# First MLP product on quarters of the matmul array, with the layer norm's mean and variance products beside the out-projection

## The chip, the cores and the metric

The kernel runs on one core of one Trainium2 chip. The metric is the device time of one execution in microseconds (us). The kernel before takes 3813.03 us, the median of three runs (3812.64 to 3813.06).

## What is computed

Input `x` is 16 images of 192 channels on 64 by 64 pixels, float32 throughout. Only the last part of the reference bears on the change. Before it, a channel norm, a 1x1 projection to 384 channels, a depthwise 3x3 convolution, four directional scans along rows and columns, a second 3x3 convolution and a sigmoid gate make `mixed`, and batch statistics are taken over it. Then:

```python
mixed = gelu(batch_norm(mixed))                      # exact gelu, not the tanh form
x = x + conv1x1(mixed, out_proj_w, out_proj_b)       # 192 -> 192
h2 = ln2d(x, ln2_w, ln2_b)                           # mean and variance over the 192 channels of each pixel
m = gelu(conv1x1(h2, fc1_w, fc1_b))                  # 192 -> 768
x = x + conv1x1(m, fc2_w, fc2_b)                     # 768 -> 192
pooled = x.mean(axis=(2, 3))                         # per image and channel
taps = squeeze_excite(pooled)                        # four 3x3 taps per image and channel
out = depthwise_conv(x, taps) + bias
```

## The kernel before

The work falls into stages. A first stage reads `x`, norms it and projects it (L484 to L518). A second one does the scans and the convolutions by channel groups (L618 to L697). The third, which the change is about, runs from about 1334 us of the profile to the end.

**Chunks.** Images are taken in pairs, eight pairs in all. A pair is cut into 8 chunks of 512 pixels (8 rows), so there are 64 chunks. Each image of a pair has its own half of the 128 partitions: partitions 0 to 63 hold 64 channels of the one image, 64 to 127 the same channels of the other, and a third index `t` (0, 1, 2) counts the three blocks of 64 channels. `HALF` are the two halves.

**The order is written out by hand.** `manual_schedule` leaves each engine's instructions in the order in which the code emits them. The loop at L1036 runs `n` from -3 to 64, and its body works on several chunks at once: the MLP of chunk n, the layer norm of chunk n+1, the out-projection of chunk n+2, the gelu after batch norm of chunk n+3. For a chunk in the middle, TensorE gets these blocks:

- `first(n, k)`, k = 0, 1, 2 (L922): two of the six blocks of 128 hidden channels. Each output `pf` is two PSUM banks of 512 columns, one for each image. For each `t` there are two matmuls, one for each image: 64 contraction rows by 128 output columns (L930). ScalarE then applies gelu to both banks at once (L933).
- `out_proj(n + 2, t)`, t = 0, 1, 2 (L857): four matmuls of 64 rows by 64 columns (L865) and four of 128 rows by 64 columns (L869), each on 256 columns of data. VectorE adds bias and residual (L872), and at t = 1 and t = 2 it sums the three channel blocks into `sm` (L876, L883, L885), so that the mean takes a contraction over 64 and not over 192.
- `second(n, k)` (L936): 128 rows by 64 columns (L827, in the helper `both`), into three banks of tag `f2`.
- `mean` (L887), called by `center(n + 1)` as `ps_m` and by `normalize(n + 1)` as `ps_v`: four matmuls of 64 by 64 (L892) with a matrix that holds 1/192.

In the trace each matmul of the code has two records; 24 records are a block of `first` or `second`, 8 are one of L865, L869 or L892.

The sequence on TensorE in one turn of the loop is: first 0, out_proj 0, second 2 of the chunk before, `ps_m`, first 1, out_proj 1, second 0, `ps_v`, first 2, out_proj 2, second 1.

**Buffers.** `pf`, `ps_o`, `ps_m` and `ps_v` share the tag `f1`, which has two buffers of two PSUM banks each. They alternate, so a block that writes one waits for the readers of the one before the last. There are 11 such tiles in a turn.

**The other engines.** `center` subtracts the mean (VectorE, L901), `squares` squares on ScalarE (L908) and sums over the channel blocks on VectorE (L909, L883, L885), `normalize` takes the square root on ScalarE (L918), the reciprocal (L919) and the product (L920) on VectorE. `final` adds the MLP's result to the image (L951). `unmix` transposes blocks (L239), `bn_gelu` is L854 and L855. Of a pair that has ended, `pooled`, `squeeze` and `excite` make the taps, and 12 `piece`s (one L990 on ScalarE, three L65 on VectorE, one output transfer each) do its convolution, two in a turn, during six of the next pair's eight chunks. Gelu and square root need different tables of ScalarE: the trace has a table load before each L918 and another before the L933 that follows.

Of the kernel before, what the change touches and what calls it, by code (L numbers as in the profile page):

```python
# [21 lines left out]
F32 = mybir.dt.float32  # L22
AF = mybir.ActivationFunctionType
# [8 lines left out]
CH = 512  # L32
HCH = CH // 2
CR = CH // HW
# [21 lines left out]
def conv_block_kernel(ctx: ExitStack, tc: tile.TileContext, x, prm, w_in, w_out, w_fc1, b_fc1, w_fc2, w1, bn1, w2, out):  # L56
    nc = tc.nc
# [5 lines left out]
    HALF = (slice(0, 64), slice(64, 128))  # L63
# [25 lines left out]
    eps6 = cp.tile([128, 1], F32, tag="eps6", name="eps6")  # L89
# [7 lines left out]
    wf1 = k2.tile([128, 3, NFC * 128], F32, tag="wf1", name="wf1")  # L97
# [6 lines left out]
    b1 = k2.tile([RED, 4], F32, tag="b1", name="b1")  # L104
    s1 = k2.tile([RED, 1], F32, tag="s1", name="s1")
    pv = k2.tile([128, 2, NPRM], F32, tag="pv", name="pv")

    mean64 = k2.tile([128, 64], F32, tag="mean64", name="mean64")
# [137 lines left out]
    with ExitStack() as stage:  # L246
# [3 lines left out]
        lo = slice(0, 64)  # L250
# [289 lines left out]
        for dst, src in ((pt3, prm), (w0, w_in)):  # L540
            v = src.rearrange("(t p) n -> p t n", p=64)
# [254 lines left out]
    k3 = ctx.enter_context(tc.tile_pool(name="k3", bufs=1))  # L796
# [12 lines left out]
    ys = {n // 2: spare[:, (n - 2) * 3 * CH:n * 3 * CH].rearrange("p (t w e) -> p t w e", t=3, w=2) for n in range(2, NCH, 2)}  # L809
    ys[0] = y_low  # L810

    pool2 = k3.tile([128, 3, 2], F32, tag="pool2", name="pool2")

    hp2 = ctx.enter_context(tc.tile_pool(name="h2", bufs=2))
    wp = ctx.enter_context(tc.tile_pool(name="w2", bufs=1))
    op = ctx.enter_context(tc.tile_pool(name="o2", bufs=2))
    ps2 = ctx.enter_context(tc.tile_pool(name="ps2", bufs=1, space=PSUM))

    n_ch = n_pairs * NCH
    NPS = NFC // 2  # L820
    st = [dict() for _ in range(n_ch)]
# [7 lines left out]
    def img_of(n):  # L829
        r = 1 + (n % NCH) * CR  # L830
        return ximg[(n // NCH) % n_img][:, :, r:r + CR, 1:1 + HW]

    def rows(a):
        return a.rearrange("p (h w) -> p h w", w=HW)
# [19 lines left out]
        nc.scalar.activation(mx[:, 0:2], mx[:, 0:2], AF.Gelu, bias=bn_bi[:, 0:1], scale=bn_sc[:, 0:1])  # L854
        nc.scalar.activation(mx[:, 2], mx[:, 2], AF.Gelu, bias=bn_bi[:, 1:2], scale=bn_sc[:, 1:2])  # L855

    def out_proj(n, t):  # L857
        s, img = st[n], img_of(n)

        ps = ps2.tile([128, 2, CH], F32, tag="f1", name="ps_o", bufs=2)[:, :, 0:CH // 2]  # L860
        cols = lambda a: a.rearrange("p r (k w) -> p r k w", k=2)

        for wh, qr in enumerate(HALF):
            for i, q in enumerate(HALF):
                nc.tensor.matmul(ps[q, wh], wo2[qr, 64 * t:64 * t + 64], s["mx"][qr, 2, 256 * i:256 * i + 256],  # L865
                                 start=True, stop=False)
        for wh in range(2):
            for i, q in enumerate(HALF):
                nc.tensor.matmul(ps[q, wh].rearrange("p (r w) -> p r w", w=32), wo[:, 64 * t:64 * t + 64],  # L869
                                 cols(rows(s["mx"][:, i]))[:, :, wh], start=False, stop=True)  # L870
        for wh in range(2):
            nc.vector.scalar_tensor_tensor(cols(img[:, t])[:, :, wh], ps[:, wh].rearrange("p (r w) -> p r w", w=32),  # L872
                                           pt3[:, t, OUTB:OUTB + 1], cols(rows(s["x2"][:, t]))[:, :, wh], ALU.add, ALU.add)
        if t == 1:
            s["sm"] = hp2.tile([128, 3, HCH], F32, tag="sm", name="sm", bufs=1)
            nc.vector.tensor_add(rows(s["sm"][:, 0:2].rearrange("p k n -> p (k n)")), img[:, 0], img[:, 1])  # L876
        if t == 2:
            sm = s["sm"]
            sums(*(rows(a) for a in (sm[:, 0], sm[:, 2], sm[:, 0], sm[:, 1])), img[:, 2, 0:CR // 2], img[:, 2, CR // 2:CR])

    def sums(o0, o1, a0, a1, b0, b1):

        nc.vector.tensor_add(o0, a0, b0)  # L883
        for i, q in enumerate(HALF):
            nc.vector.tensor_add(o1[HALF[1 - i]], a1[q], b1[q])  # L885

    def mean(name, s0, s1):  # L887

        ps = ps2.tile([128, 2, CH], F32, tag="f1", name=name, bufs=2)[:, :, 0:HCH]
        for k, a in enumerate((s0, s1)):  # L890
            for i, q in enumerate(HALF):
                nc.tensor.matmul(ps[HALF[i ^ k], k], mean64[q], a[q], start=True, stop=True)  # L892
        return ps

    def center(n):
        s, img = st[n], img_of(n)
        pm = mean("ps_m", s["sm"][:, 0], s["sm"][:, 2])
        h = hp2.tile([128, 3, CH], F32, tag="h2", name="h2")
        hr = CR // 2
        for k in range(2):  # L900
            nc.vector.tensor_sub(h.rearrange("p t (h w) -> p t h w", w=HW)[:, :, k * hr:(k + 1) * hr], img[:, :, k * hr:(k + 1) * hr],  # L901
                                 rows(pm[:, k]).unsqueeze(1).broadcast_to([128, 3, hr, HW]))
        s.update(h=h)

    def squares(n):
        s = st[n]
        sq = wp.tile([128, 3, CH], F32, tag="sq2", name="sq2")
        nc.scalar.activation(sq, s["h"], AF.Square)  # L908
        nc.vector.tensor_add(sq[:, 0], sq[:, 0], sq[:, 1])  # L909
        v = sq.rearrange("p t (k n) -> p t k n", k=2)  # L910
        sums(v[:, 0, 0], v[:, 1, 0], v[:, 0, 0], v[:, 0, 1], v[:, 2, 0], v[:, 2, 1])
        s.update(sq=v)

    def normalize(n):
        s = st[n]
        pw = mean("ps_v", s["sq"][:, 0, 0], s["sq"][:, 1, 0])
        rs = hp2.tile([128, CH], F32, tag="rs2", name="rs2", bufs=1)
        nc.scalar.activation(rs.rearrange("p (k n) -> p k n", k=2), pw, AF.Sqrt, bias=eps6)  # L918
        nc.vector.reciprocal(rs, rs)  # L919
        nc.vector.tensor_mul(s["h"], s["h"], rs.unsqueeze(1).broadcast_to([128, 3, CH]))  # L920

    def first(n, k):  # L922

        s = st[n]
        s["gl", k] = []
        for m in (2 * k, 2 * k + 1):
            pf = ps2.tile([128, 2, CH], F32, tag="f1", name="ps_f1", bufs=2)
            for t in range(3):
                for i, q in enumerate(HALF):
                    nc.tensor.matmul(pf[:, i], wf1[q, t, 128 * m:128 * m + 128], s["h"][q, t],  # L930
                                     start=(t == 0), stop=(t == 2))
            gl = wp.tile([128, 2, CH], F32, tag="gl", name="gl", bufs=4)
            nc.scalar.activation(gl, pf, AF.Gelu, bias=bf1[:, m:m + 1])  # L933
            s["gl", k].append(gl)
# [48 lines left out]
    def dynamic(p, g, t):  # L983
        xi, taps, r = ximg[p % n_img], pst[p]["taps"], g * GR
        o = op.tile([128, GR, HW], F32, tag="o", name="o")
        for k in range(NTAP):
            src = xi[:, t, r + k // 3:r + k // 3 + GR, k % 3:k % 3 + HW]
            w = taps[:, t, k:k + 1]
            if k == 0:
                nc.scalar.activation(o, src, AF.Identity, bias=pt3[:, t, BIAS:BIAS + 1], scale=w)  # L990
            else:
                stt(o, src, w, o)
        for i, q in enumerate(HALF):
            nc.gpsimd.dma_start(ov[2 * p + i, 64 * t:64 * t + 64, r * HW:(r + GR) * HW], o[q].rearrange("p h w -> p (h w)"))  # L994
# [31 lines left out]
    def at(f, n, *a):  # L1026
        if n is not None and 0 <= n < n_ch:
            f(n, *a)
# [3 lines left out]
    def piece():  # L1032
        if pieces:
            dynamic(*pieces.pop(0))

    for n in range(-3, n_ch + 1):  # L1036
        ended = (n - 1) // NCH if n >= NCH and (n - 1) % NCH == NCH - 1 else None
        if n + 5 < NCH and (n + 5) % 2 == 0:
            load_y(n + 5, ys[(n + 5) // 2], (nc.sync, nc.gpsimd) if n == -3 else (nc.gpsimd,))
        if n == -3:  # L1040
            border(ximg[0])
        if n == 0:
            nc.vector.memset(pool2, 0.0)
        if n == NCH - 3:
            border(ximg[1])

        early_, late_ = (n + 3, None) if n != -1 else (None, 2)
        at(load, n + 3)
        at(unmix, early_)
        at(load_mixed, n + 4)  # L1050
        at(first, n, 0)
        at(bn_gelu, early_)
        at(out_proj, n + 2, 0)
        piece()
        at(second, n - 1, NPS - 1)
        at(center, n + 1)
        at(final, n - 1)
        if ended is not None:
            pooled(ended)
        at(first, n, 1)  # L1060
        if ended is not None:
            squeeze(ended)
        at(out_proj, n + 2, 1)
        at(squares, n + 1)
        at(second, n, 0)
        piece()
        at(normalize, n + 1)
        at(first, n, 2)
        if ended is not None:
            excite(ended)  # L1070
            if ended < n_pairs - 1:
                pieces += [(ended, g, t) for g in range(NG) for t in range(3)]
        at(out_proj, n + 2, 2)
        at(second, n, 1)
        at(unmix, late_)
        at(bn_gelu, late_)
# [64 lines left out]
```

## Time and profile before

| what | value |
|---|---|
| span of the profiled execution | 3814.8 us |
| TensorE busy with matmuls | 3764.5 us (99%), 25,644 matmul records |
| weight loads (beside the matmuls) | 1719.9 us (45%) |
| VectorE busy | 2665.5 us (70%) |
| ScalarE busy | 1779.2 us (47%) |
| first MLP product, L930 | 4,608 records, 1050.2 us |
| second MLP product, L827 | 4,608 records, 1021.6 us |
| out-projection, L869 and L865 | 1,536 records each, 210.0 and 129.9 us |
| mean and variance products, L892 | 512 records each, 43.0 and 43.7 us |

Busy time is the time in which at least one instruction of the engine (or of the group) was running. Matmuls overlap, so a busy TensorE is not yet TensorE at its peak; how far apart the starts of successive matmuls are tells more. "idle before" in a group's row is the time in which the engine had nothing running just ahead of the group's instructions.

### The profile page before, as it was taken

How to read it: one execution, taken by the hardware profiler on the slowest of the kernel's cores; microseconds unless marked ns; L12 is line 12 of the kernel's file. 1: busy time of each engine (PE TensorE's matmuls, PEld its weight loads, DVE VectorE, ACT ScalarE, POOL GpSimd, SP SyncE). 2: the span in 40 equal slices, each digit the busy share in tenths (PEclk: the TensorE clock that was granted, in tenths of full speed). 3: DMA queues.
4: the chain of work that ended last, by engine and by line, in shares of the span. 5: the costliest groups of instructions: out<-in, count | busy, mean ns of one | idle time of the engine just before them, and what ended most of it. 6: DMA issues, size and time to landing. Idle time of an engine off the chain costs nothing.

```text
span 3814.8 us, 61825 instructions
## 1 busy us (share of the span) xinstructions
PE 3764.5 (99%) x25644; PEld 1719.9 (45%) x25644; DVE 2665.5 (70%) x4132; ACT 1779.2 (47%) x1881; POOL 420.1 (11%) x683
## 2 busy tenths in 40 slices
PE   8999999999999899999999999999999999999998
PEld 5666656555555433333333333333333333333333
DVE  6887776999999964557656656756665765674753
ACT  3433434888888733333434333433433433343433
POOL 2434332010110110000000000000000000000000
PEclk9999999999999999999999999999999999999999
DMA  6899998999999741112212212222222221221212
GB/s 163 239 252 237 272 275 261 282 280 273 284 275 269 208 89 34 43 39 72 75 48 61 75 56 64 61 67 58 70 56 64 72 65 45 76 71 42 67 36 72
DMA packets 308391, 491.15 MB, mean 129 GB/s; under 512 B 46656, under 2 KB 202640, under 8 KB 308112
## 3 DMA queue, kind: packets, MB, share of 16 engines
q1 hardware_dynamic: 250064, 295.14, 29.2%
q0 software_dynamic: 57152, 190.94, 18.9%
q8 instruction: 203, 3.33, 0.4%
q10 hardware_dynamic: 896, 1.12, 0.1%
q14 instruction: 76, 0.62, 0.1%
HBM read 284.91 MB, written 197.92 MB: 127 GB/s over the span
## 4 chain that ended last, share of the span: by engine, by line
PE 96%; DMA 1%; DVE 1%; ACT 0%; issue 0%; POOL 0%; SPq 0%; ACTq 0%; POOLq 0%
PE ps_f L930 27%; PE ps_f L827 26%; PE ps_pj L512 13%; PE ps_l L662 11%; PE ps_d L618 6%; PE ps_o L869 5%; PE ps_o L865 3%; PE ps_xt L484 2%; PE ps_v L892 1%; PE ps_m L892 1%; DMA xa<-in_x_dram 1%; PE ps_k L827 0%; DMA ximg<-mixed_d 0%; DMA mixed_d<-mid 0%; DVE v L653 0%
## 5 line engine op out<-in xcount | busy, mean ns | idle before, releaser
L930 PE MATMUL ps_f<-h,wf 64*128 64x512 f32 x4608 | 1050.2, 601 | 4.0 <-DVE h L920 3.3
L827 PE MATMUL ps_f<-gl,place 128*64 128x512 f32 x4608 | 1021.6, 592 | 0.0
L933 ACT ACTIVATE gl<-ps_f,bf 128x1024 f32<-128x1024 f32 x384 | 427.6, 1114 | 1163.7 <-PE ps_f L930 1162.9
L930 PEld LDWEIGHTS ps_f<-h,wf 64*128 64x128 f32 x4608 | 434.3, 187 | 563.0 <-issue 560.8
L872 DVE SCALAR_TENSOR_TENSOR ximg<-ps_o,pt,low 128x256 f32<-128x256 f32 x384 | 168.3, 480 | 626.5 <-PE ps_o L869 623.7
L827 PEld LDWEIGHTS ps_f<-gl,place 128*64 128x64 f32 x4608 | 330.7, 137 | 579.8 <-issue 537.6
L512 PE MATMUL ps_pj<-wi,xa 64*128 64x384 f32 x3072 | 516.0, 489 | 4.9 <-DVE stg L517 4.8
L65 DVE SCALAR_TENSOR_TENSOR o<-ximg,taps,o 128x1024 f32<-128x1024 f32 x252 | 323.7, 1285 | 85.9 <-ACT o L990 78.4
L512 PEld LDWEIGHTS ps_pj<-wi,xa 64*128 64x128 f32 x3072 | 293.6, 188 | 199.3 <-issue 12.8
L994 POOL DMA_DIRECT2D out_dram<-o x168 | 87.9, 528 | 2134.3 <-DVE o L65 2131.5
L919 DVE RECIPROCAL rs<-rs 128x512 f32<-128x512 f32 x64 | 214.3, 3348 | 64.9 <-ACT rs L918 64.9
L653 DVE TENSOR_TENSOR_SCAN v<-tab,q 128x1024 f32<-128x1024 f32 x96 | 218.3, 2274 | 7.5 <-DMA pg_d<-mid 7.5
L655 DVE TENSOR_TENSOR_SCAN v<-tab,q 128x1024 f32<-128x1024 f32 x96 | 217.5, 2266 | 0.0
L869 PE MATMUL ps_o<-low,wo 128*64 128x256 f32 x1536 | 210.0, 395 | 0.0
L518 ACT ACTIVATE stg<-ps_pj,rsa 128x384 f32<-128x384 f32 x128 | 120.0, 941 | 191.3 <-PE ps_pj L512 179.8
L641 ACT ACTIVATE tab<-mask,dec_b 128x1024 f32<-128x1024 f32 x192 | 209.0, 1137 | 0.0
L518 ACT ACTIVATE mid<-ps_pj,rsa 128x384 f32<-128x384 f32 x128 | 120.7, 943 | 180.9 <-PE ps_pj L512 175.0
L901 DVE TENSOR_TENSOR h<-ximg,ps_m 128x768 f32<-128x768 f32 x128 | 116.1, 948 | 98.7 <-PE ps_m L892 98.7
L491 DVE BATCH_NORM_STATS2 st<-ps_xt 128x6 f32<-128x192 f32 x512 | 173.2, 338 | 17.0 <-PE ps_xt L484 16.8
L239 DVE STREAM_TRANSPOSE low<-low 128x512 f32<-128x512 f32 x174 | 167.7, 1015 | 2.0 <-issue 0.3
L472 POOL DMA_DIRECT2D xa<-in_x_dram x192 | 119.8, 630 | 363.1 <-PE ps_pj L512 285.1
L951 DVE SCALAR_TENSOR_TENSOR ximg<-ps_f,pt,ximg 128x512 f32<-128x512 f32 x192 | 134.0, 747 | 36.2 <-PE ps_f L827 35.8
(198 smaller groups left out, 4020.0 us busy)
## 6 DMA issues: line engine op xcount, KB each, us to landing
low<-in_x_dram SPq DMA_DIRECT2D x128, 384.0 KB
out_dram<-o POOLq DMA_DIRECT2D x168, 256.0 KB, 3.7
mid<-pg_d SPq DMA_DIRECT2D x8, 4096.0 KB
low<-mixed_d SPq DMA_DIRECT2D x116, 256.0 KB
low<-pg_d SPq DMA_DIRECT2D x7, 4096.0 KB
pg_o<-pg_d SPq DMA_DIRECT2D x7, 4096.0 KB
xa<-in_x_dram POOLq DMA_DIRECT2D x192, 128.0 KB, 5.8
xa<-in_x_dram SPq DMA_DIRECT2D x192, 128.0 KB
```

The source lines that it names most:

```text
L65: nc.vector.scalar_tensor_tensor(o, in0, scalar, in1, ALU.mult, ALU.add, **kw)
L512: nc.tensor.matmul(ps[i], pixels(n, t, g)[q], wi[q, t].rearrange("p g k c -> p (g k c)"), start=(t == 0), stop=(t == 2))
L518: nc.scalar.activation(stag[blk][1][:, :, j], ps[1], AF.Copy, scale=rs[:, g, 1:2])
L618: nc.tensor.matmul(dst(ps[o, ih]), mats[g % 2]["dm"][q, di + 1, :, ch], src(s["pg"][q, :, 0, ch]), start=(di == 0), stop=stop)
L653: nc.vector.tensor_tensor_scan(vf, tab, q, 0.0, ALU.mult, ALU.add)
L655: nc.vector.tensor_tensor_scan(vf[:, ::-1], tab[:, ::-1], q[:, ::-1], 0.0, ALU.mult, ALU.add)
L662: nc.tensor.matmul(dst(bst[k]["ps"][i][o]), lm_of(g)[q, m, :, c], src(q, ih), start=start, stop=stop)
L827: nc.tensor.matmul(ps[q], w(i), rhs(i), start=start, stop=stop)
L869: nc.tensor.matmul(ps[q, wh].rearrange("p (r w) -> p r w", w=32), wo[:, 64 * t:64 * t + 64], cols(rows(s["mx"][:, i]))[:, :, wh], start=Fa ...
L919: nc.vector.reciprocal(rs, rs)
L930: nc.tensor.matmul(pf[:, i], wf1[q, t, 128 * m:128 * m + 128], s["h"][q, t], start=(t == 0), stop=(t == 2))
L933: nc.scalar.activation(gl, pf, AF.Gelu, bias=bf1[:, m:m + 1])
```

## The change

The first MLP product, the mean and the variance are put into one form with the first half of the out-projection: 64 rows by 64 columns, four of them on the four quarters of the array. The mean and the variance are placed directly before the out-projection's quarters, and each shares a PSUM tile with it (the mean or variance in the upper 256 columns, the out-projection in the lower), so that three blocks of the same form follow each other. Since the tile is shared, both are read only when both are written. The layer norm's mean is taken one place earlier in the turn, and the variance before second(n, 0) and not after it. The sums that feed them are cut into four parts of 64 partitions, laid out for the quarters. After the square root, an activation of one column calls gelu, so that gelu's table is fetched before it is needed.

```diff
+    warm = k3.tile([128, 1], F32, tag="warm", name="warm")
-        ps = ps2.tile([128, 2, CH], F32, tag="f1", name="ps_o", bufs=2)[:, :, 0:CH // 2]
+    def products(n, t):
+        if not -2 <= n < n_ch - 1:
+            return
+        ps = ps2.tile([128, 2, CH], F32, tag="f1", name="ps_o", bufs=2)
+        pm, po = ps[:, :, HCH:CH], ps[:, :, 0:HCH]
+        if t < 2:
+            at(mean, n + 1, pm, ("sm", "sq")[t])
+        at(out_proj, n + 2, t, po)
+        if t == 0:
+            at(center, n + 1, pm)
+        if t == 1 and 0 <= n + 1 < n_ch:
+            st[n + 1]["pw"] = pm
+        at(residual, n + 2, t, po)
...
-        nc.vector.tensor_add(o0, a0, b0)
-        for i, q in enumerate(HALF):
-            nc.vector.tensor_add(o1[HALF[1 - i]], a1[q], b1[q])
+        lo, hi = HALF
+        for o, a, b in ((o0[lo], a0[lo], b0[lo]), (ox[lo], a0[hi], b0[hi]), (ox[hi], a1[lo], b1[lo]), (o1[hi], a1[hi], b1[hi])):
+            nc.vector.tensor_add(o, a, b)
...
-        ps = ps2.tile([128, 2, CH], F32, tag="f1", name=name, bufs=2)[:, :, 0:HCH]
-        for k, a in enumerate((s0, s1)):
-            for i, q in enumerate(HALF):
-                nc.tensor.matmul(ps[HALF[i ^ k], k], mean64[q], a[q], start=True, stop=True)
-        return ps
+        s0, s1, sx = st[n][what]
+        for k, kinds in enumerate(((s0, sx), (sx, s1))):
+            for i, a in enumerate(kinds):
+                nc.tensor.matmul(ps[HALF[i], k], mean64[HALF[k]], a[HALF[k]], start=True, stop=True)
...
-        pw = mean("ps_v", s["sq"][:, 0, 0], s["sq"][:, 1, 0])
...
+        nc.scalar.activation(rs.rearrange("p (k n) -> p k n", k=2), s["pw"], AF.Sqrt, bias=eps6)
+        nc.scalar.activation(warm, eps6, AF.Gelu)
...
-                    nc.tensor.matmul(pf[:, i], wf1[q, t, 128 * m:128 * m + 128], s["h"][q, t],
-                                     start=(t == 0), stop=(t == 2))
+                    for j, o in enumerate(HALF):
+                        m0 = 128 * m + 64 * j
+                        nc.tensor.matmul(pf[o, i], wf1[q, t, m0:m0 + 64], s["h"][q, t], start=(t == 0), stop=(t == 2))
...
         at(first, n, 0)
         at(bn_gelu, early_)
-        at(out_proj, n + 2, 0)
+        products(n, 0)
         piece()
+        at(squares, n + 1)
         at(second, n - 1, NPS - 1)
-        at(center, n + 1)
         at(final, n - 1)
...
         at(first, n, 1)
+        products(n, 1)
...
-        at(out_proj, n + 2, 1)
-        at(squares, n + 1)
         at(second, n, 0)
         piece()
         at(normalize, n + 1)
...
-        at(out_proj, n + 2, 2)
+        products(n, 2)
         at(second, n, 1)
```

In the turn after the change TensorE's sequence is: first 0, mean, out_proj 0, second 2 of the chunk before, first 1, variance, out_proj 1, second 0, first 2, out_proj 2, second 1. The tag `f1` has nine tiles in a turn.

## Prediction before the changed kernel was run

> **What bounds the kernel now.** I read the shares by engine first, then the chain of waits, then the costliest groups: TensorE is busy 99%, is 96% of the chain, and the groups of the last stage hardly idle. Nothing waits, so what is left to gain is the rate within the busy time.
>
> ```profile
> PE 3764.5 (99%) x25644; PEld 1719.9 (45%) x25644; DVE 2665.5 (70%) x4132; ACT 1779.2 (47%) x1881; POOL 420.1 (11%) x683
> PE 96%; DMA 1%; DVE 1%; ACT 0%; issue 0%; POOL 0%; SPq 0%; ACTq 0%; POOLq 0%
> L930 PE MATMUL ps_f<-h,wf 64*128 64x512 f32 x4608 | 1050.2, 601 | 4.0 <-DVE h L920 3.3
> L827 PE MATMUL ps_f<-gl,place 128*64 128x512 f32 x4608 | 1021.6, 592 | 0.0
> ```
>
> For the rate I took the timeline of TensorE in a middle chunk (start, length, records). Starts of neighbouring rows give each block's true length; the lengths in the rows overlap.
>
> ```profile
> 2527.63 5.42 PE L930 MATMUL ps_f<-h,wf 64*128 64x512 f32 x24
> 2532.98 0.66 PE L865 MATMUL ps_o<-low,wo 64*64 64x256 f32 x8
> 2533.57 1.08 PE L869 MATMUL ps_o<-low,wo 128*64 128x256 f32 x8
> 2534.49 5.32 PE L827 MATMUL ps_f<-gl,place 128*64 128x512 f32 x24
> 2539.74 0.66 PE L892 MATMUL ps_m<-sm,mean 64*64 64x256 f32 x8
> 2540.33 0.70 PE L930 MATMUL ps_f<-h,wf 64*128 64x512 f32 x2
> ```
>
> Blocks: L930 5.35 us, L865 0.59, L869 0.92, L827 5.25, L892 0.59. Single records show the grain: two matmuls (halves) or four (quarters) start within 20 ns, and the next group follows after 0.429 us at 512 columns, 0.2155 at 256. So 24 records in halves are 12 groups, 5.15 us; eight in quarters two groups, 0.43; eight in halves four, 0.86. The rest sits at **changes of form** only. The first group of a new form comes about 0.10 us late (0.11 after a 256-column group). The second comes late again, by 0.052 where the new form has 64 columns (0.267, not 0.215), by 0.105 where it has 128 (0.534, not 0.429). L869 to L827 changes line, not form, and costs nothing.
>
> A chunk has 11 changes: L930 to L865 three at 0.148 us (0.096+0.052), L865 to L869 three at 0.163, L827 to L892 two at 0.152, L892 to L930 two at 0.216, L827 to L930 one at 0.205. Sum 1.874. Add 36+36 groups of 0.429 and 22 of 0.2155: 35.63. Together 37.50. The period is 37.55 us in 14 of 61 middle chunks, 37.73 in 40, 39.25 in the 7 that also run squeeze and excite. The missing bits are two waits: 0.05 us of L865 on the gelu behind a table load, and in the 40 chunks with pieces 0.17 us of L930's second tile on center (L901). The first is visible here, gelu ending at 2520.81 and L865 at 2520.87, 0.05 later than its pattern:
>
> ```profile
> 2518.41 1.28 ACT L933 ACT_TABLE_LOAD   x1 [2.11 <-PE ps_f L930]
> 2519.70 1.11 ACT L933 ACTIVATE gl<-ps_f,bf 128x1024 f32<-128x1024 f32 x1
> 2520.87 0.66 PE L865 MATMUL ps_o<-low,wo 64*64 64x256 f32 x8
> ```
>
> **What the Trainium skill says.** "TensorEngine Tiling (Array Packing)", section Key Properties: changing the tiling mode, not just the tile, drains TensorE. The trace agrees, at 0.10 us. "TensorE: Matmul & The Clock Gate", section LDWEIGHTS: a load takes its columns divided by 1.2 ns, 53 ns for 64 and 107 for 128. The second group's lag of 52 and 105 ns is just that, so I read it as a weight load with no matmul to hide behind. "ScalarE: Activation LUTs", section What ACT_TABLE_LOAD costs: some 1283 ns a load; the trace has 1.28 us.
>
> **The change, part by part.**
>
> *First product on quarters.* 2,304 matmuls become 4,608 (9,216 records, 30,252 in all), in groups of four instead of two: the same 36 groups a chunk. Their price stands in the stage before, where L662 does 64x64 by 512 in quarters. Six groups in 2.57 us (four of them of 504 columns) and four in 1.71 are 0.428 each, also across a change of line:
>
> ```profile
> 1208.92 2.75 PE L662 MATMUL ps_l<-q,mid 64*64 64x512 f32 x24
> 1211.49 1.90 PE L662 MATMUL ps_l<-v,mid 64*64 64x512 f32 x16
> 1213.20 2.79 PE L618 MATMUL ps_d<-mid,dm 64*64 64x512 f32 x40
> ```
>
> So: no gain and no loss within the block. The doubled loads lie beside matmuls, as L662's do.
>
> *Changes of form.* First, mean and L865 now have one form. Left are L865 to L869 three times at 0.163 and L827 to first three times at 0.10+0.052=0.152 (the price of L827 to L892): 0.945 us instead of 1.874. Gain 0.93 a chunk.
>
> *Waits removed.* The table load moves behind the square root, where ScalarE would idle some 5 us (square root done at 22.0 in the count below, next gelu at 27.5): gain 0.05. The one-column activation (nearest row 0.29 us) hides there too. Center is now followed by second (5.25) and the first tile of first (2.6) before its buffer is wanted: gain 0.17 in 40 chunks.
>
> *Waits added.* Center and residual (VectorE), and the square root (ScalarE), stand until out_proj's end, up to 1.5 us later than the mean or variance alone. Counting from first 0's start in a chunk with pieces: mean 5.20, L865 5.63, L869 6.17, second 7.09. Center (1.81) runs 7.3 to 9.1, residual (0.88) to 10.0, a piece (3.93) to 13.95; ScalarE does two gelus, bn_gelu, the piece's L990 (to 9.5) and the square (1.47, to 11.0). The sums (0.69 + four of 0.42) end at 16.35, and the variance wants them at 17.55: 1.2 us of slack. Queued behind are final (to 18.8; second wants its banks from 19.4), residual 1 and the second piece (to 25.1), reciprocal 3.35 and product 1.76 (to 30.3; the next first wants h at 36.6). `f1` tiles: out_proj's wait for gelus that end 1.2 us ahead, first's for residuals further ahead. All hidden, the variance by least.
>
> *Four-part sums.* Four of 0.42 us instead of 0.43+0.84, twice a chunk: +0.43 each, 55 us more VectorE over all, in the slack just counted.
>
> A middle chunk is then 35.63+0.945=36.58 us, to the 37.55, 37.73 or 39.25 of before. Gains: 14x0.97=13.6, 40x1.15=46.0, and for the seven (36.58+1.65 for squeeze and excite) 7x1.02=7.1. The last two chunks, which have no out-projection, give 0.6. Sum 67.3.
>
> *Start of the stage,* where no MLP hides the chain from sum to first product. Before, the mean ran at 1342.5 us and the first product began at 1356.81. After: sums 0.43 longer, the mean followed by out_proj (1.5) before center may start; squares likewise 0.43 longer, the variance followed by another out_proj (1.5), and residual 1 ahead of the reciprocal. That shifts the first product by 3.6 us. One table load (1.28) then no longer precedes bn_gelu: about +2.3 remains. Between 2 and 5; I take +3.5, with chunk 0 counted in and its gain left out.
>
> Forecast: 3813.0-67.3+3.5=**3749.2 us**.
>
> **Rivals.** (a) *The variance waits.* If sums come 2 us later than counted (pieces held by output buffers, transposes by loads), the slack of 1.2 is overdrawn by 0.8 in 40 chunks: +32, 3781. For it: smallest slack, long VectorE queue. Against: VectorE is busy only about 65% here. (b) *Only part of the drain goes.* If second-group loads stay exposed at the joins first to mean and first to out_proj, five of 0.052 in 64 chunks: +17, 3766. Against: L662 to L618 joins at 0.428. (c) *Slower.* If in this code the four loads of a group don't hide, each of 36 groups takes 0.052 more: 1.87 a chunk, 120 us, 3869. Against: L662 again, though its weights are laid out otherwise. (d) *Quicker:* the start costs nothing and squeeze changes form less often: 3743.
>
> **How the numbers follow.** Forecast 0.70, (a) 0.10, (b) 0.08, (c) 0.05, (d) 0.07. The range, 3741 to 3770, takes in the forecast with the start's bounds, (b) and (d), and a mild (a). Faster by over 0.2% (below 3805.4): all but (c) and a heavy (a), 0.94; the same 0.01; slower 0.05.
>
> **What would show it.** First at 0.429 a group in fours, block 5.20; mean and L865 0.2155 a group with no lag before them; six lags a chunk; period 36.6 for pieces and none alike; no table load ahead of L933. A TensorE wait on the sums of squares would show (a), groups of 0.48 us (c).

## The result, and the profile after

The changed kernel takes 3756.72 us (median of 4 runs, 3752.6 to 3758.05), against 3813.05 for the kernel before beside it (median of 4, 3812.64 to 3823.58). The medians lie 56 us apart. The ratio, into which every run goes, is 0.9844, with a 95% interval of 0.9825 to 0.9863. The forecast was 3749.2, the range 3741 to 3770. In a second comparison, in which both kernels ran slower, the changed kernel took 3763.53 us, the kernel before 3822.01, and the ratio was 0.9841 (0.9825 to 0.9857).

Medians carry the first two stages, which the change does not touch and which vary: the first out-projection begins between 1331.28 and 1341.10 us in the twelve profiles of this study, all with the same code ahead of it. Why they vary is open. Below, therefore, I compare pieces of the third stage from the traces; there the 61 middle chunks together repeat to within 0.01 us in the profiles that have the same code for them.

The page of the changed kernel, its busy times and costliest groups:

```profile
PE 3696.1 (99%) x30252; PEld 1651.4 (44%) x30252; DVE 2716.6 (72%) x4260; ACT 1794.8 (48%) x1945; POOL 420.2 (11%) x683
L955 PE MATMUL ps_f<-h,wf 64*64 64x512 f32 x9216 | 1035.9, 595 | 6.8 <-DVE h L943 6.7
L828 PE MATMUL ps_f<-gl,place 128*64 128x512 f32 x4608 | 1022.2, 592 | 0.0
```

TensorE is as busy as before, 99%, with 4,608 records more and 68 us less. The first product (now L955) has twice the records in 14 us less. Most of the gain is not in these rows; it is between the blocks. The timeline of TensorE in a middle chunk (start, length, records):

```profile
2535.49 5.38 PE L955 MATMUL ps_f<-h,wf 64*64 64x512 f32 x48
2540.69 0.61 PE L916 MATMUL ps_o<-sm,mean 64*64 64x256 f32 x8
2541.12 0.61 PE L883 MATMUL ps_o<-low,wo 64*64 64x256 f32 x8
2541.66 1.08 PE L887 MATMUL ps_o<-low,wo 128*64 128x256 f32 x8
2542.58 5.32 PE L828 MATMUL ps_f<-gl,place 128*64 128x512 f32 x24
2547.83 5.38 PE L955 MATMUL ps_f<-h,wf 64*64 64x512 f32 x48
```

By the differences of the starts: first 5.20 us (5.35 before), mean 0.43 (0.59), L883 0.54 (0.59), L887 0.92, second 5.25. Single records show first's groups of four 0.429 us apart, the mean's following in 0.216, and lags only where second turns to first (0.529, then 0.480) and L883 to L887 (0.326, then 0.267): six a chunk.

Where the time went, between fixed points of the two traces (us):

| stretch | before | after | difference |
|---|---|---|---|
| start of the span to first out-projection | 1334.10 | 1331.28 | -2.82 (code unchanged) |
| first out-projection to first MLP product | 22.71 | 30.16 | +7.45 |
| chunk 0 | 35.93 | 34.97 | -0.96 |
| chunks 1 to 61 | 2309.83 | 2243.24 | -66.59 |
| last two chunks, to the last second product | 69.72 | 69.16 | -0.56 |
| the rest | 42.47 | 41.99 | -0.48 |

### The profile page after: what moved, and what is told of

Its sections match the earlier page's. It is cut to its first block, busy times and chain, and to the rows that moved or that the text cites. A ratio compares the mean times of both kernels' runs of the same rounds, so it can differ in the third digit from the quotient of the medians.

```text
span 3750.8 us, 71230 instructions
## 1 busy us (share of the span) xinstructions
PE 3696.1 (99%) x30252; PEld 1651.4 (44%) x30252; DVE 2716.6 (72%) x4260; ACT 1794.8 (48%) x1945; POOL 420.2 (11%) x683
## 4 chain that ended last, share of the span: by engine, by line
PE 97%; DVE 1%; DMA 1%; ACT 0%; issue 0%; SPq 0%; ACTq 0%; POOL 0%; DVEq 0%
PE ps_f L955 27%; PE ps_f L828 26%; PE ps_pj L512 13%; PE ps_l L662 11%; PE ps_d L618 7%; PE ps_o L887 5%; PE ps_xt L484 2%; PE ps_o L883 2%; PE ps_o L916 2%; DMA xa<-in_x_dram 1%; PE ps_k L828 0%; DVE v L653 0%; DVE v L655 0%; DMA out_dram<-ol 0%; PE ps_d L1038 0%
## 5 line engine op out<-in xcount | busy, mean ns | idle before, releaser
L955 PE MATMUL ps_f<-h,wf 64*64 64x512 f32 x9216 | 1035.9, 595 | 6.8 <-DVE h L943 6.7
L955 PEld LDWEIGHTS ps_f<-h,wf 64*64 64x64 f32 x9216 | 334.5, 133 | 693.8 <-issue 642.6
L923 DVE TENSOR_TENSOR h<-ximg,ps_o 128x768 f32<-128x768 f32 x128 | 116.4, 951 | 425.5 <-PE ps_o L887 417.2
L893 DVE SCALAR_TENSOR_TENSOR ximg<-ps_o,pt,low 128x256 f32<-128x256 f32 x384 | 168.0, 480 | 267.5 <-PE ps_o L887 264.9
L65 DVE SCALAR_TENSOR_TENSOR o<-ximg,taps,o 128x1024 f32<-128x1024 f32 x252 | 323.2, 1282 | 8.7 <-ACT o L1014 2.6
L887 PE MATMUL ps_o<-low,wo 128*64 128x256 f32 x1536 | 210.2, 395 | 0.0
```

Source lines behind the costliest of these rows:

```text
L65: nc.vector.scalar_tensor_tensor(o, in0, scalar, in1, ALU.mult, ALU.add, **kw)
L955: nc.tensor.matmul(pf[o, i], wf1[q, t, m0:m0 + 64], s["h"][q, t], start=(t == 0), stop=(t == 2))
```

## The experiments

Times are medians. "Chunks" is the stretch of chunks 1 to 61 in the profile, "start" the one from first out-projection to first MLP product. Intervals are those of the ratio to the kernel before, run beside it. Compare by ratio: the kernel before took 3817.99 us beside `quarters_only`, `move_only`, `twice_the_changes` and `own_tile`, 3822.01 beside `no_early_table`, `early_table_only`, `start_apart` and the repeat, and 3817.24 beside `quarters_and_table`.

| kernel | us | ratio (95%) | chunks | start |
|---|---|---|---|---|
| before | 3813.05 | 1 | 2309.83 | 22.71 |
| changed | 3756.72 | 0.9844 (0.9825 to 0.9863) | 2243.24 | 30.16 |
| quarters_only | 3783.16 | 0.9916 (0.9900 to 0.9933) | 2278.12 | 22.24 |
| early_table_only | 3817.48 | 0.9987 (0.9980 to 0.9993) | 2307.05 | 22.23 |
| quarters_and_table | 3770.47 | 0.9867 (0.9844 to 0.9890) | 2265.43 | 22.67 |
| move_only | 3797.31 | 0.9947 (0.9931 to 0.9964) | 2279.98 | 29.81 |
| no_early_table | 3773.94 | 0.9872 (0.9857 to 0.9887) | 2255.57 | 31.41 |
| twice_the_changes | 3814.77 | 0.9992 (0.9985 to 0.9998) | 2299.79 | 32.17 |
| own_tile | 3890.71 | 1.0189 (1.0174 to 1.0204) | 2376.87 | 27.27 |
| start_apart | 3755.44 | 0.9822 (0.9808 to 0.9837) | 2243.24 | 24.32 |
| start_mean_apart | 3754.45 (one run) | none taken | 2243.24 | 29.41 |
| changed, again | 3763.53 | 0.9841 (0.9825 to 0.9857) | 2243.24 | 31.62 |

### Is it the number of changes of form?

`twice_the_changes` is the changed kernel with the out-projection's two parts exchanged:

```diff
-        for wh, qr in enumerate(HALF):
-            for i, q in enumerate(HALF):
-                nc.tensor.matmul(ps[q, wh], wo2[qr, 64 * t:64 * t + 64], s["mx"][qr, 2, 256 * i:256 * i + 256],
-                                 start=True, stop=False)
...
-                                 cols(rows(s["mx"][:, i]))[:, :, wh], start=False, stop=True)
+                                 cols(rows(s["mx"][:, i]))[:, :, wh], start=True, stop=False)
+        for wh, qr in enumerate(HALF):
+            for i, q in enumerate(HALF):
+                nc.tensor.matmul(ps[q, wh], wo2[qr, 64 * t:64 * t + 64], s["mx"][qr, 2, 256 * i:256 * i + 256],
+                                 start=False, stop=True)
```

> The changed kernel with the two parts of the out-projection in the other order: first the matmuls of 128 rows by 64 columns, then the quarters. The same matmuls, and 12 changes of form a chunk in place of 6. Theory: 0.163 + 0.152 us more at each of three places, 0.945 us a chunk in 62 chunks: 59 us more than the changed kernel, about 3816, no gain left over the kernel before. Rival (the gain is in the waits that fell away, not in the form): about 3757.

The chunks grew by 56.55 us, 0.927 a chunk where 0.945 were counted, and the gain over the kernel before was nearly gone. The matmuls are the same; six more changes of form cost some 0.154 us each. The timeline of TensorE shows where they lie:

```profile
2508.04 5.38 PE L955 MATMUL ps_f<-h,wf 64*64 64x512 f32 x48
2513.24 0.61 PE L916 MATMUL ps_o<-sq,mean 64*64 64x256 f32 x8
2513.78 1.08 PE L883 MATMUL ps_o<-low,wo 128*64 128x256 f32 x8
2514.80 0.66 PE L887 MATMUL ps_o<-low,wo 64*64 64x256 f32 x8
2515.39 5.37 PE L828 MATMUL ps_f<-gl,place 128*64 128x512 f32 x24
2520.69 5.38 PE L955 MATMUL ps_f<-h,wf 64*64 64x512 f32 x48
```

By the starts, the halves, now between two quarter blocks, take 1.02 us and not 0.92, the quarters 0.59 and not 0.54, second 5.30 and not 5.25, the variance 0.54 and not 0.43.

### One part alone

`quarters_only` is the kernel before with this edit:

```diff
-                    nc.tensor.matmul(pf[:, i], wf1[q, t, 128 * m:128 * m + 128], s["h"][q, t],
-                                     start=(t == 0), stop=(t == 2))
+                    for j, o in enumerate(HALF):
+                        m0 = 128 * m + 64 * j
+                        nc.tensor.matmul(pf[o, i], wf1[q, t, m0:m0 + 64], s["h"][q, t], start=(t == 0), stop=(t == 2))
```

> The kernel before with the first product on quarters and nothing else moved. Theory (a change of form costs 0.15 to 0.22 us, a change of block in the same form nothing): the mean and variance blocks, out of place as they are, now have the form of the blocks behind them, so six changes a chunk are left, as in the changed kernel: 0.93 us a chunk less. In the 40 chunks with pieces the 0.22 us won between mean and first are lost again in the wait on center, since VectorE sets its end. 21x0.93 + 40x0.71 + 0.5 = 48 us: about 3765. The start of the stage stays as before. Rival 1 (the mean and variance have to stand beside the out-projection for the gain): only first to out-projection and second to first get cheaper, 0.60 us a chunk: about 3776. Rival 2 (each change of block costs, whatever the form): about 3810.

Measured 3783, and 31.7 us won in the chunks where I expected 48. The total lies near that of rival 1, but the blocks speak against it. All the changes of form went that the theory names: from mean to first it takes 0.48 us and not 0.59, so that lag is gone, and the kernel has six changes a chunk. But two waits, and the lags behind them, took most of 25 us of the 57 (61 times the 0.93 of the expectation) back. The largest of TensorE's waits in the third stage (total, times, longest):

```profile
PE ps_f L932 <- DVE h L901: 11.5, 40, 0.6
```

It is first's second tile waiting for center, 40 times; the blocks tell its full size, since the last matmuls still run while it begins. One such chunk (first 1 in its two tiles of 24 records, then the out-projection; most rows of the other engines are left out):

```profile
2633.70 3.93 DVE L65 SCALAR_TENSOR_TENSOR o<-ximg,taps,o 128x1024 f32<-128x1024 f32 x3 [1.87 <-ACT o L991]
2636.47 2.75 PE L932 MATMUL ps_f<-h,wf 64*64 64x512 f32 x24
2637.55 1.81 DVE L901 TENSOR_TENSOR h<-ximg,ps_m 128x768 f32<-128x768 f32 x2
2639.51 2.81 PE L932 MATMUL ps_f<-h,wf 64*64 64x512 f32 x24 [0.28 <-DVE h L901]
2642.10 0.64 PE L865 MATMUL ps_o<-low,wo 64*64 64x256 f32 x8
```

In chunks with pieces VectorE comes to center only after a piece (L65), whose own start hangs on the gelus of first 0, so that nearly everything TensorE saves from first 0 to first 1 (0.148 and 0.216 us) is waited away: first 1 took 5.63 us there, not 5.15 (before 5.52, not 5.35), and the out-projection behind it 0.03 more. The second loss does not show among the waits at all: the third first block took 5.33 us, not 5.15, until the gelu behind its table load was done, and the out-projection after it 0.05 more.

`early_table_only` and `quarters_and_table` add to the kernel before, and to `quarters_only`, these lines:

```diff
+    warm = k3.tile([128, 1], F32, tag="warm", name="warm")
...
+        nc.scalar.activation(warm, eps6, AF.Gelu)
```

> The kernel before with the one-column gelu after the square root and nothing else. Theory: 0.05 us less in 61 chunks and 1.28 us less at the start of the stage: 4.3 us faster than the kernel before, about 3809. Rival: no difference.

> The kernel before with the first product on quarters and the one-column gelu after the square root; mean and variance stay where they were. Theory (without the lag of a change of form behind first's third block, the late table costs some 0.23 us a chunk and not 0.05; the wait on center in chunks with pieces stays): from chunk 1 to chunk 62 2278.1 us of the kernel with quarters alone become 2266, between 2262 and 2268; that kernel in all about 12 us faster. Rival (the table is worth 3 us here, as in the halves): 2275.

In halves the early table is worth 2.8 us over the chunks, in quarters 12.7, both as expected; the third first block is 5.15 us again. `no_early_table` takes those lines out of the changed kernel:

> The changed kernel without the one-column gelu after the square root. Theory: the load of gelu's table stands ahead of the first gelu after first's third block again; the out-projection waits 0.05 us for it in some 61 chunks, 3.0 us, and batch norm's gelu at the start of the stage gets its 1.28 us back: 4.3 us slower than the changed kernel run beside it. Rival (the one-column activation only fills idle time of ScalarE): no difference.

It lost 12.3 us in the chunks and not 3: 0.23 in each of 54 chunks, and nothing in the seven with squeeze and excite. I had priced the late table by what it cost before, 0.05 us; there the lag of the change of form ran at the same time and covered most of the wait. With the change gone, the wait stands bare: first 2 takes 5.38 us, not 5.20, and the out-projection behind it 0.59, not 0.54.

`move_only` is the changed kernel with the two `first` lines of `quarters_only` put back:

> The changed kernel with the first product in halves of 64 rows by 128 columns again. Theory: nine changes a chunk: first to mean or out-projection 3x0.148, out-projection's two parts 3x0.163, second to first 3x0.205, 1.55 us; no wait on center or gelu. A chunk is 37.18 us: 30 us won over the chunks, of which the longer start of the stage (7.4 us, less 1.3) takes 6: about 3789. Rival (the gain is in sharing the tile and in the place of the mean): most of the 56 us, about 3760.

29.9 us won in the chunks against 30 counted, in all 3797 against 3789; the medians of this comparison are all some 5 us higher (the kernel before 3818 beside it).

One after the other the parts give: quarters 31.7, early table 12.7, mean and variance moved 22.2, together 66.6 us. The last step removes no change of form. It removes the waits on center: in `quarters_and_table` the 40 chunks with pieces take 37.09 us and those without 36.58, in the changed kernel both take 36.58, which is 20 of the 22 us. The rest is in the seven chunks with squeeze and excite (38.50 and 38.25 us). The move does two things at once: the mean comes one place earlier on TensorE, and center comes ahead of the piece on VectorE. Which of the two removes the wait was not run apart.

### Is sharing the tile needed?

`own_tile` gives mean and variance a tile of their own:

```diff
-        ps = ps2.tile([128, 2, CH], F32, tag="f1", name="ps_o", bufs=2)
-        pm, po = ps[:, :, HCH:CH], ps[:, :, 0:HCH]
-        if t < 2:
+        pm = None
+        if t < 2 and 0 <= n + 1 < n_ch:
+            pm = ps2.tile([128, 2, CH], F32, tag="f1", name="ps_m", bufs=2)[:, :, 0:HCH]
             at(mean, n + 1, pm, ("sm", "sq")[t])
+        ps = ps2.tile([128, 2, CH], F32, tag="f1", name="ps_o", bufs=2)
+        po = ps[:, :, 0:HCH]
```

> The changed kernel with mean and variance in a PSUM tile of their own, so that center and the square root need not wait for the out-projection. Theory (sharing saves a buffer): with 11 tiles in a turn on two buffers the out-projection has to wait for the gelu of the first product's second tile, which ends some 1.4 us after that product; 0.97 us idle at t=0 and t=1, 1.95 us a chunk in 62 chunks, less some 2 us at the start of the stage: about 3876, slower than before. Rival (reading only when all is written costs something in every chunk): a bit faster than the changed kernel, 3745 to 3755.

3891 us, slower than the kernel before. TensorE:

```profile
2532.18 0.61 PE L918 MATMUL ps_m<-sm,mean 64*64 64x256 f32 x8
2533.66 0.66 PE L885 MATMUL ps_o<-low,wo 64*64 64x256 f32 x8 [0.86 <-ACT gl L959]
2534.25 1.08 PE L889 MATMUL ps_o<-low,wo 128*64 128x256 f32 x8
```

The out-projection starts 1.48 us after the mean, not 0.43: it waits for the gelu of the tile before the mean's. That is 1.05 us, and 0.05 more in the block itself (0.59 for 0.54), twice a chunk: 2.19 us a chunk, 1.95 expected. Reading both only when both are written costs nothing in a chunk (the changed kernel's blocks keep their counted lengths there); two more tiles in a turn on the same two buffers do.

### Why the start grew

At the start of the stage nothing hides the chain from sums to first product. ScalarE there, first the kernel before, then the changed one:

```profile
1346.00 1.48 ACT L908 ACTIVATE sq<-h 128x1536 f32<-128x1536 f32 x1 [9.25 <-PE ps_o L869]
1347.50 1.28 ACT L918 ACT_TABLE_LOAD   x1
1350.80 0.69 ACT L918 ACTIVATE rs<-ps_v,eps 128x512 f32<-128x512 f32 x1 [2.01 <-PE ps_v L892]
```

```profile
1345.19 1.48 ACT L930 ACTIVATE sq<-h 128x1536 f32<-128x1536 f32 x1 [11.26 <-DVE h L923]
1354.13 1.28 ACT L939 ACT_TABLE_LOAD   x1 [7.46 <-DVE ximg L893]
1355.43 0.69 ACT L939 ACTIVATE rs<-ps_o,eps 128x512 f32<-128x512 f32 x1
```

Before, the square root's table was loaded right after the square, while VectorE summed. Now the load stands until VectorE's residual has read the same tile, and then lies bare ahead of the square root. VectorE, again the kernel before first:

```profile
1348.73 0.85 DVE L885 TENSOR_TENSOR sq<-sq 64x256 f32<-64x256 f32 x2
1351.52 3.35 DVE L919 RECIPROCAL rs<-rs 128x512 f32<-128x512 f32 x1 [1.94 <-ACT rs L918]
```

```profile
1343.26 1.82 DVE L923 TENSOR_TENSOR h<-ximg,ps_o 128x768 f32<-128x768 f32 x2 [2.19 <-PE ps_o L887]
...
1347.44 1.77 DVE L908 TENSOR_TENSOR sq<-sq 64x256 f32<-64x256 f32 x4
1353.18 0.88 DVE L893 SCALAR_TENSOR_TENSOR ximg<-ps_o,pt,low 128x256 f32<-128x256 f32 x2 [3.97 <-PE ps_o L887]
1354.09 0.69 DVE L897 TENSOR_TENSOR sm<-ximg 128x512 f32<-128x512 f32 x1
1356.15 3.35 DVE L942 RECIPROCAL rs<-rs 128x512 f32<-128x512 f32 x1 [1.37 <-ACT rs L939]
```

From the end of the sums (1349.21) to the reciprocal it is 6.94 us, against 1.94 before: 3.97 until variance and out-projection are done, 0.9 for the residual, 1.28 for the load, 0.7 for the square root. Center begins 2.2 us after its sums, against 0.8 before.

Two causes lie in this, and `own_tile` tells them apart, for it leaves the order of the changed kernel and only gives mean and variance tiles of their own. There ScalarE loads the table right behind the square again (two rows of ScalarE, then two of VectorE):

```profile
1347.40 1.48 ACT L932 ACTIVATE sq<-h 128x1536 f32<-128x1536 f32 x1 [9.93 <-DVE h L925]
1348.90 1.28 ACT L941 ACT_TABLE_LOAD   x1
...
1355.27 0.88 DVE L895 SCALAR_TENSOR_TENSOR ximg<-ps_o,pt,low 128x256 f32<-128x256 f32 x2 [3.76 <-PE ps_o L889]
1356.79 3.35 DVE L944 RECIPROCAL rs<-rs 128x512 f32<-128x512 f32 x1
```

So the bare load comes of the shared tile. The larger part does not: the reciprocal still begins 5.28 us after the sums (1351.51), because VectorE has the residual of the out-projection ahead of it in its order. `start_apart` changes both, the tile and the order, for chunk 0 alone:

```diff
+        alone = n == -1 and t < 2
+        if alone:
+            pm = ps2.tile([128, 2, CH], F32, tag="f1", name="ps_m", bufs=2)[:, :, 0:HCH]
+            mean(0, pm, ("sm", "sq")[t])
+            if t == 0:
+                center(0, pm)
+            else:
+                st[0]["pw"] = pm
+                normalize(0)
         ps = ps2.tile([128, 2, CH], F32, tag="f1", name="ps_o", bufs=2)
...
-        at(normalize, n + 1)
+        at(normalize, n + 1 if n >= 0 else None)
```

> The changed kernel, with mean and variance of chunk 0 in tiles of their own, centered and normalized before the out-projection of chunk 1 that stands beside them; all later chunks share tiles as before. Theory (the start of the stage grew by 7.4 us because center and square root wait for out-projections that no MLP hides, and because the table of the square root is loaded only after the residual): the first MLP product begins some 7 us earlier after the first out-projection, 23 us and not 30; 6 us faster than the changed kernel, about 3750. Rival (what is longer is hidden behind batch norm's gelu of chunk 2): no difference.

The start fell to 24.32 us, and ScalarE loads the table beside the sums again:

```profile
1353.41 1.48 ACT L941 ACTIVATE sq<-h 128x1536 f32<-128x1536 f32 x1 [9.66 <-DVE h L934]
1354.92 1.28 ACT L950 ACT_TABLE_LOAD   x1
1358.63 0.69 ACT L950 ACTIVATE rs<-ps_m,eps 128x512 f32<-128x512 f32 x1 [2.43 <-PE ps_m L927]
```

From the first out-projection to the end it takes 2413.64 us, the changed kernel 2419.52 and 2420.87: 6 to 7 us less. The medians, 3755.44 and 3763.53, say 8, though the intervals of the two ratios overlap. Counted from the first out-projection on, it is the fastest of these versions. `start_mean_apart` does the mean's half only:

> The changed kernel, with only the mean of chunk 0 in a tile of its own and centered ahead of chunk 1's first out-projection; its variance shares a tile as in the changed kernel. Theory: of the 7.4 us by which the start (first out-projection to first MLP product) grew, 2.0 are the wait of center and come back, 5.0 are the variance's (out-projection, residual and table load ahead of the square root) and stay: 28.2 us, beside 30.2 to 31.6 of the changed kernel. Rival (the mean's wait is all of it): 23 us.

29.41 us. From the start of center to the first MLP product it takes 18.18 us, as in the changed kernel (before: 12.73), so the 5.4 us of the variance's part stay. Center's wait after the sums fell from 2.2 us to 0.7. The total came out 1.2 us above the 28.2 expected: the sums were ready 0.7 us later after the first out-projection in this run, and center got back 1.5 us and not 2.0.

`after_again` is the changed kernel once more:

> The changed kernel once more, beside the three others: for its own spread, and to see in which stage the runs differ. Theory: the stages ahead of the change vary by some us from run to run of any kernel; from the first out-projection on the traces agree within 1 us.

The chunks agree to 0.01 us, all from the first out-projection on to 1.35 us, and not to the 1 us expected. Nearly all of it is in the start: center there waits 3.83 us in the repeat and 2.19 in the first profile, since the out-projection ahead of it runs slower (its rows of 128 by 64 take 1.89 us, not 1.08).

## Why the prediction was right

**Rate in quarters: right.** 0.429 us a group, as L662's row had it. The doubled records cost nothing. Rival (c) falls.

**Six changes of form for eleven: right,** and with it the chunks: 66.59 us measured, 66.7 predicted for chunks 1 to 61 (13.6+46.0+7.1). The blocks came out as priced, 5.20, 0.43, 0.54, 0.92 and 5.25 us. Rival (b) falls: at the joins within a form nothing lags. `twice_the_changes` shows the cause: the same matmuls with six changes more lose the gain. But the step's picture of which edit does what was too coarse: the changes go with the quarters alone, and the three blocks need not stand together for it (`quarters_only` has six as well). The move is worth 22 us for another reason, mainly the wait on center. That the lag of a second group is a weight load with nothing to hide it is supported and not shown: the load rows of the kernel before take some 131 ns for 64 columns and 187 for 128, so that only their difference, 56 ns, is near that of the two lags, 53.

**Waits removed: right as a sum, mis-sized as a part.** The late table was put at 0.05 us a chunk. Beside the quarters it is worth 0.23 in 54 chunks (`no_early_table`), because the change of form had covered it. The total did not suffer only because change and wait both went.

**Waits added: right.** The waits of TensorE in the third stage of the changed kernel, past the start:

```profile
PE ps_t L991 <- DVE pool L985: 1.4, 1, 1.4
PE ps_d L1038 <- ACT ol L1040: 0.9, 1, 0.9
PE ps_d L1038 <- PE ps_k L828: 0.8, 1, 0.8
PE ps_k L828 <- DVE red L994: 0.6, 1, 0.6
```

Four single waits, none on center, sums or gelu in any middle chunk, and chunks with pieces take 36.58 us like those without: rival (a) falls. I had not seen that the square root would also wait for the residual; in a chunk it lies in slack.

**Start of the stage: this step failed.** It was priced at +3.6 us, +2.3 after batch norm's gelu had its table load back, at most 5, and entered as +3.5 with chunk 0's gain left out. Measured: +7.45 in the start, -0.96 in chunk 0, so 6.5 net (8.0 in the repeat). Rival (d), that the start costs nothing, falls with it. The sum itself is not clear: the terms named for the 3.6 us (0.43 and 1.5 twice, and a residual of 0.88) add up to 4.7. The part of the mean was about right, center's start after its sums growing from 0.8 to 2.2 us. The terms that were too small are the two behind the variance. TensorE there, the kernel before first:

```profile
1348.84 1.48 PE L892 MATMUL ps_v<-sq,mean 64*64 64x256 f32 x6 [2.86 <-DVE sq L883]
...
1351.53 1.97 PE L869 MATMUL ps_o<-low,wo 128*64 128x256 f32 x8
```

```profile
1348.00 1.95 PE L916 MATMUL ps_o<-sq,mean 64*64 64x256 f32 x6 [4.79 <-DVE sq L908]
...
1351.16 1.97 PE L887 MATMUL ps_o<-low,wo 128*64 128x256 f32 x8
1353.06 0.66 PE L883 MATMUL ps_o<-low,wo 64*64 64x256 f32 x8
```

First, variance and out-projection were done 4.0 us after the sums, where mean and out-projection a little earlier had taken 2.2: the out-projection ran at half rate (L887 took 1.90 us there, 0.92 in a chunk). The kernel before had shown it, its L869 in the same place running 1.97 us. The Trainium skill, "TensorE: Matmul & The Clock Gate", Part 1, says that an idle window of some 3.4 us sets the array's clock to half. The traces agree in the clock and not in the idle time: 0.50 was granted from 1346.26 to 1353.09 us, over both blocks and from 3.1 us into a gap of 4.79; but in the kernel before it was granted from 1348.08, 2.1 us into a gap of 2.86, and in the repeat from 1343.20, after a gap of only 1.52. How much idle time it takes stays open. Second, the square root's table load (1.28) was taken as hidden and is not, since it waits for VectorE's read of the shared tile. The skill, "PSUM — Partial Sum Buffer", section PSUM bank collisions raise a hardware error, says that two engines in one bank and quadrant at once raise an error, reads at different addresses included; the wait in the trace (7.46 us, released by L893) is an order that keeps them apart. `own_tile` and `start_apart`, where the square root has its own tile, have no such wait.

**The number:** it fell inside the range because the chunks, by far its largest term, came out as counted. From the first out-projection to the end the traces give 61.1 us of gain (59.8 in the repeat), where the forecast has 63.8; the start makes nearly all of that difference. The median lies 7.5 us above the forecast. The other 4 to 5 us are not in the traces of the third stage; the stages ahead of it vary by more than that from profile to profile, and which run fell where the medians do not tell.

## What to carry to other kernels

Where TensorE is busy 99%, look at the distances between the starts of matmuls, and count where their form (rows by columns) changes: each change costs 0.15 to 0.22 us here, whether lines change or not. Before taking a lag away, ask which wait it covers: here a table load of 0.05 us a chunk became one of 0.23, and a wait on center of 0.17 us became 0.48. And look at the stretch before the steady loop separately, since an order that is free inside it can lie bare there, at another clock.

## What the runs showed of the hardware that I had not expected

After a stall of TensorE the second group lags as it does after a change of form. In `own_tile` the out-projection that waited for a gelu takes 0.59 us, 0.05 more than without the wait, though its form is that of the mean before it, and so does the one in `no_early_table`. Its eight weight loads begin together with its first matmul there (2533.65 us in `own_tile`), while the mean's first ones, which nothing held up, stand 0.4 us ahead. So the lag seems to belong to a restart with no weights loaded ahead, and not to the change itself.

An ACT_TABLE_LOAD can stand behind a wait: in the kernel before that of gelu behind the product's matmuls (2.11 us, in the prediction's lines), in the changed kernel that of the square root behind L893. It need not: at the start of the kernel before and of `own_tile` the load of the square root ran ahead, and the square root alone waited for the variance. Why gelu's load had to wait there and that of the square root did not is open. A one-column activation, 0.20 us long, brought gelu's load forward here and freed it of the wait.

The granted clock fell to half after 1.5 to 3.1 us of idle TensorE in three profiles of the start of the stage, and the first block of first in chunk 0 ran partly at it (7.8 us in the changed kernel, 5.2 in a middle chunk).
